# Less VectorE code in a branch that isn't taken, and another order of the first steps, in a gated cross-attention and mixture-of-experts kernel

## Chip, cores and metric

One core of a Trainium2 chip. The metric is the time of one launch in microseconds (us), the median of several runs. A core has five engines with a queue of instructions each: TensorE (PE, its weight loads PEld), VectorE (DVE), ScalarE (ACT), GpSimd (POOL) and SyncE (SP, which here only starts transfers). Waits between queues go over semaphores.

## What is computed

Eight batches of 256 rows, 512 wide. Each batch has a memory of 256 rows, of which a mask leaves some. The rows of x, normalized, attend to the memory they are left with; the result, times a gate, is added to x. Then each row goes, normalized again, to the two best of eight experts.

```
scores = einsum('bsd,bmd->bsm', layernorm(x), memory) / sqrt(D)
attn = softmax(where(mask, scores, -1e30))
x = x + tanh(g_xattn) * einsum('bsm,bmd->bsd', attn, memory)
t = layernorm(x)
probs = softmax(t @ w_router.T); top 2 of 8, weights made to sum to 1
out = sum over the two: (silu(t @ w_gate.T) * (t @ w_up.T)) @ w_down.T
x = x + tanh(g_ffn) * out
```

In these inputs a mask leaves at most 64 of a memory's 256 rows.

## The kernel before

Rows are worked in 16 tiles of 128 (NT), two to a batch; memories in four pairs of batches (NP). Matrix operands are float32.

**The start.** `m_find` numbers the unmasked rows of every memory by matmuls with a triangle of ones. For a pair p, `m_hot(p)` (VectorE, L216) makes a one-hot matrix of those numbers, `m_pick(p)` (TensorE, L224) turns it into row indices in the bank pidx, and `m_fetch(p)` (L228 on VectorE, L229 on GpSimd) adds an offset, giving gid, and gathers 2 x 64 rows of the memory into cns[p]. `m_count` finds the longest memory. Three matmuls into a bank that nobody reads (L586) keep TensorE at work.

**The branch.** All five engines load that count (L587) and branch (L589). If a memory has more than 64 rows, `long_way` handles all batches with whole memories, tile by tile and without overlap: a block of straight code on each engine. Else three loads of x are started, after ScalarE has read the gathered rows once (L594). Near the program's start, `mark_branch_hint_location` (L571) puts an instruction into the queues of TensorE and VectorE that names the branch's target in advance.

**Pairs.** `m_mean` (statistics on VectorE, L175), `m_centre` (ScalarE, L265) and `m_turn` (TensorE L272, ScalarE L273) make a pair's centred, transposed memory cT. `m_route(p)` (TensorE L279; ScalarE L281 to L283) makes the memory's router logits cw and scales cns.

**The loop over steps** (L603) is a pipeline written out by hand: each engine runs its instructions in the order in which the functions are called. In step s: `a_probs` of tile s-1 (transposed probabilities: TensorE, then ScalarE L378), `f_centre` of s-2, `a_stats` of tile s+3 (VectorE), in even steps `a_scale` (one power on GpSimd, L351), `a_scores` of tile s (TensorE L359, VectorE L363, ScalarE L366), then `a_values` of s-1 (TensorE L387, L389; VectorE L390 to L395: router logits, best two, and the sum into x). Behind follow ranking and bookkeeping of finished pairs of tiles: `f_mark`, `f_rank` (TensorE into the bank rank, VectorE, and four products ac on GpSimd, L456), `f_table` (TensorE into the bank table, L463), `f_count`, `f_weigh` (a transfer of finished rows to HBM). rank and table are started by one matmul each (L625, L626) and added to until the end of the loop. Step 0 holds extra work: the indices and gathers of pairs 1 to 3, scores of tile 1, `m_route(0)`, statistics of tiles 2 and 3, the masks `m_hide` and the constants of later steps on GpSimd.

**The banks.** Tiles of the PSUM pool share eight banks. A bank goes to a tile at its first write in the order of the program, and comes free with its last use.

**The experts.** When all rows are ranked, GpSimd gathers them by expert in lists of 128 (L677), and each list runs through its expert's matrices on TensorE (L183, L695, L710, L719); results are scattered to HBM by GpSimd (L682).

## Time and profile before

| | us |
|---|---|
| median of 3 runs | 300.76 (300.16 to 301.12) |
| the profiled execution | 298.97 |
| its span, first to last instruction | 297.2 |
| routing stage, to the first gather by expert | 92.4 |
| TensorE busy in 0 to 92.4 / 92.4 to 202 / 202 to 297.2 | 71.7 / 104.4 / 87.0 |
| VectorE busy in the same | 64.9 / 37.0 / 30.8 |
| ScalarE | 51.2 / 35.3 / 28.4 |
| GpSimd | 54.3 / 43.8 / 52.6 |

The second half of the table is from the windows of the profile. A row of the timeline below reads: start, duration, engine, line, operation, output <- inputs, shape, count, and in brackets how long the engine had been idle and who released it. Starts are counted from the first instruction. A letter q behind an engine's name (DVEq) means its queue: branches, register loads, semaphores, DMA starts.

### The profile page before, as it was taken

The page shows a single profiled execution, that of the slowest core. Times are in us where ns is not written, and L with a number is a line of the kernel's source. Part 1 is how long each engine was busy: PE and PEld are TensorE (multiplying, and loading weights), DVE is VectorE, ACT ScalarE, POOL GpSimd, SP SyncE. Part 2 cuts the span into 40 slices and gives each one's busy share as a digit, 9 for nine tenths or more (in the row PEclk, how much of TensorE's full clock was granted, in tenths as well). Part 3 has the DMA queues.
Part 4 walks back from the last instruction along what each step waited for, and adds up shares of the span by engine and source line. Part 5 has one row for each costly group of instructions (what it writes and reads, how often), then busy time and mean ns, then how long its engine had stood idle before and what let it go on. Part 6 is the DMA issues. An engine that isn't in the chain of part 4 may idle for free. (4 is left out here: it accounts for less than half of the span.)

```text
span 297.2 us, 4010 instructions
## 1 busy us (share of the span) xinstructions
PE 263.1 (89%) x1106; PEld 165.1 (56%) x1106; DVE 132.8 (45%) x450; ACT 114.8 (39%) x275; POOL 150.6 (51%) x239
## 2 busy tenths in 40 slices
PE   5587779989861999999999999999998999999990
PEld 4175568777641565555555555555554555555540
DVE  2438888887771123333333333332304334242441
ACT  2124667777770233333333333332204233333320
POOL 4528955647574403444444444443764847475252
PEclk9979999999995799999999999999999999999996
DMA  4589967999434702323323323331762655553322
GB/s 146 186 302 417 310 210 256 299 334 337 163 149 147 221 3 75 88 104 121 105 86 100 126 92 116 105 123 51 215 201 78 204 174 157 152 169 128 106 78 99
DMA packets 16078, 48.55 MB, mean 163 GB/s; under 512 B 3182, under 2 KB 3182, under 8 KB 16049
## 3 DMA queue, kind: packets, MB, share of 16 engines
q0 software_dynamic: 7984, 25.64, 27.3%
q1 hardware_dynamic: 5888, 17.85, 18.1%
q10 hardware_dynamic: 2176, 4.72, 4.1%
q8 instruction: 13, 0.21, 0.3%
q14 instruction: 17, 0.13, 0.1%
HBM read 35.08 MB, written 14.68 MB: 167 GB/s over the span
## 5 line engine op out<-in xcount | busy, mean ns | idle before, releaser
L695 PE MATMUL pgu<-wgu_sb,xT_g 128*128 x304 | 105.7, 490 | 0.9 <-ACTq L768 0.9
L695 PEld LDWEIGHTS pgu<-wgu_sb,xT_g 128*128 128x128 f32 x304 | 57.8, 192 | 49.3 <-issue 17.2
L719 PE MATMUL py<-wd_sb,hT 96*128 x152 | 71.3, 592 | 0.0
L701 DVE SCALAR_TENSOR_TENSOR th<-th,pgu 128x192 f32<-128x192 f32 x38 | 13.4, 354 | 99.1 <-ACT th L700 75.4
L682 POOL DMA_INDIRECT acc_d<-y,ids x19 | 19.3, 1016 | 59.8 <-DVE y L725 57.1
L677 POOL DMA_INDIRECT xall<-xc_d,ids x38 | 37.1, 975 | 13.1 <-issue 6.1
L700 ACT ACTIVATE th<-pgu,xall 128x192 f32<-128x192 f32 x38 | 16.0, 421 | 70.1 <-PE pgu L695 56.8
L723 ACT ACTIVATE y<-py,xall 128x512 f32<-128x512 f32 x38 | 26.1, 688 | 38.6 <-PE py L719 30.4
L719 PEld LDWEIGHTS py<-wd_sb,hT 96*128 96x128 f32 x152 | 25.9, 190 | 18.7 <-issue 18.7
L185 ACT COPY xT_g<-pt_g 128x512 f32<-128x512 f32 x38 | 22.2, 585 | 28.7 <-PE pt_g L183 16.9
L682 POOL DMA_INDIRECT out<-y,ids x19 | 19.2, 1013 | 26.5 <-DVE y L732 18.3
L456 POOL TENSOR_SCALAR ac<-cols,low,idt 128x128 f32<-128x128 f32 x30 | 25.7, 865 | 11.6 <-DVE low L446 11.6
L183 PE MATMUL pt_g<-ident,xall 128*128 128x128 f32 x152 | 23.8, 281 | 6.2 <-issue 5.6
L725 DVE SCALAR_TENSOR_TENSOR y<-xall,y 128x512 f32<-128x512 f32 x19 | 14.3, 752 | 28.8 <-ACT y L723 27.3
L677 POOL DMA_INDIRECT acc<-acc_d,ids x19 | 18.5, 975 | 8.4 <-issue 8.4
L183 PEld LDWEIGHTS pt_g<-ident,xall 128*128 128x128 f32 x152 | 18.3, 144 | 7.0 <-issue 5.9
L359 PE MATMUL psc<-cT,xT 128*128 128x137 f32 x128 | 19.0, 296 | 1.3 <-issue 0.7
L359 PEld LDWEIGHTS psc<-cT,xT 128*128 128x128 f32 x128 | 17.5, 204 | 2.0 <-issue 1.2
L710 PEld LDWEIGHTS pht<-ident,h 128*96 128x96 f32 x76 | 9.5, 126 | 14.2 <-issue 7.4
L389 PE MATMUL pav<-cn,prT 128*128 128x512 f32 x32 | 16.4, 594 | 0.0
L703 DVE SCALAR_TENSOR_TENSOR h<-th,xall,pgu 128x192 f32<-128x192 f32 x38 | 15.8, 415 | 1.4
L712 DVE COPY hT<-pht 96x256 f32<-96x256 f32 x38 | 15.8, 415 | 0.3 <-PE py L719 0.2
(156 smaller groups left out, 295.6 us busy)
## 6 DMA issues: line engine op xcount, KB each, us to landing
wgu_sb<-wgu SPq DMA_DIRECT2D x8, 768.0 KB, 9.1
xc_d<-xr ACTq DMA_DIRECT2D x8, 576.0 KB, 5.9
xT<-xT SPq DMA_DIRECT2D x8, 512.0 KB, 6.8
wd_sb<-wd SPq DMA_DIRECT2D x8, 384.0 KB, 9.4
xall<-x SPq DMA_DIRECT2D x1, 2048.0 KB
xall<-x SPq DMA_DIRECT2D x2, 512.0 KB, 3.8
xall<-x SPq DMA_DIRECT2D x1, 1024.0 KB, 8.3
xall<-xc_d,ids POOLq DMA_INDIRECT x38
```

The source lines that it names most:

```text
L183: nc.tensor.transpose(pt[:, c, :], src[:, c * P:(c + 1) * P], ident)
L185: nc.scalar.copy(dst, pt)
L359: nc.tensor.matmul(both, lhsT=xTs[b][:, c, t * P:(t + 1) * P], rhs=cTs[p % 2][:, c, :], start=(c == 0), stop=(c == HC - 1))
L389: nc.tensor.matmul(pav, lhsT=prT, rhs=cns[p], start=True, stop=True)
L456: by.tensor_scalar(at_col[:, n, :], cols, low[:, n:n + 1], idt[:, i:i + 1], ALU.is_equal, ALU.mult)
L677: nc.gpsimd.indirect_dma_start(out=g, out_offset=None, in_=src[:, :], in_offset=bass.IndirectOffsetOnAxis(ap=ids[:, q:q + 1], axis=0))
L682: free(nc.gpsimd.indirect_dma_start(out=dst, out_offset=bass.IndirectOffsetOnAxis(ap=ids[:, q:q + 1], axis=0), in_=z, in_offset=None, boun ...
L695: nc.tensor.matmul(pgu, lhsT=xgT[:, c, :], rhs=wgu_sb[:, bass.ds(v * GU + c * 2 * I, 2 * I)], start=(c == 0), stop=(c == HC - 1))
L700: nc.scalar.activation(th, pgu[:, 0:I], AF.Tanh, scale=xg[:, RS:RS + 1])
L703: nc.vector.scalar_tensor_tensor(h, th, xg[:, R2:R2 + 1], pgu[:, I:2 * I], ALU.mult, ALU.mult)
L719: nc.tensor.matmul(py, lhsT=hT[:, k, :], rhs=wd_sb[:, bass.ds(v * DN + k * D, D)], start=(k == 0), stop=(k == 1))
L723: nc.scalar.activation(y, py, AF.Copy, scale=xg[:, c:c + 1])
```

## The change

Three things.

1. In `long_way`, five instructions a tile leave VectorE. The addition of epsilon and the product of the softmax's sum with the gate go to GpSimd; the normalization, the scaling of the result and the copy of the router's part go to ScalarE. For the normalization GpSimd makes a further factor, -mean times the reciprocal deviation, in two instructions. The branch hint stays on TensorE alone.
2. In step 0, `m_route(0)` stands ahead of the pairs' indices. Only pair 1 is picked and gathered in step 0, with the statistics of tile 2 between the two. Pair 2's hot matrix stays in step 0, its pick and gather move to step 1, ahead of tile 0's values, with the hot matrix of pair 3 behind them; pair 3's pick and gather move to step 2.
3. The two matmuls that start rank and table move from step 0 to step 1, behind tile 0's values, so that their banks are given out later.

```diff
-               (("l_st", 6), ("l_mv", 2), ("l_rs", 1), ("l_vg", 1), ("l_nmx", 1), ("l_den", 1))}
-        mv, rs, vg, nmx, den = (one[k] for k in ("l_mv", "l_rs", "l_vg", "l_nmx", "l_den"))
+               (("l_st", 6), ("l_mv", 2), ("l_rs", 1), ("l_vg", 1), ("l_nmx", 1), ("l_den", 1), ("l_ng", 1))}
+        mv, rs, vg, nmx, den, ng = (one[k] for k in ("l_mv", "l_rs", "l_vg", "l_nmx", "l_den", "l_ng"))
...
-                nc.vector.tensor_scalar(mv[:, 1:2], mv[:, 1:2], EPS, None, ALU.add)
+                nc.gpsimd.tensor_scalar(mv[:, 1:2], mv[:, 1:2], EPS, None, ALU.add)
                 nc.gpsimd.tensor_tensor(rs, mv[:, 1:2], expo, ALU.pow)
+                nc.gpsimd.tensor_tensor(ng, mv[:, 0:1], rs, ALU.mult)
+                nc.gpsimd.tensor_scalar(ng, ng, -1.0, None, ALU.mult)
                 xa = row([P, D], "lx")
-                nc.vector.tensor_scalar(xa, xs[i], mv[:, 0:1], rs, ALU.subtract, ALU.mult)
+                nc.scalar.activation(xa, xs[i], AF.Identity, bias=ng, scale=rs)
...
-                nc.vector.tensor_mul(den, den, vg)
+                nc.gpsimd.tensor_tensor(den, den, vg, ALU.mult)
...
-                nc.vector.tensor_scalar(more, pav, den, None, ALU.mult)
+                nc.scalar.activation(more, pav, AF.Copy, scale=den)
...
-                nc.vector.tensor_copy(xadd[:, i, :], plg)
+                nc.scalar.copy(xadd[:, i, :], plg)
...
-        tc.mark_branch_hint_location("long", engines=[PE, DVE])
+        tc.mark_branch_hint_location("long", engines=[PE])
...
                 m_hot(1)
                 m_hot(2)
                 a_scores(1)
-                for n in range(1, 3):
-                    m_pick(n)
-                    m_fetch(n)
                 m_route(0)
-                m_hot(3)
-                m_pick(3)
-                m_fetch(3)
-                nc.tensor.matmul(rank, lhsT=ones[0:1, :], rhs=lbase, start=True, stop=True)
-                nc.tensor.matmul(table.rearrange("p k r -> p (k r)"), lhsT=ones[0:1, :], rhs=zero[:, 0:2 * P], start=True, stop=True)
+                m_pick(1)
                 a_stats(2)
+                m_fetch(1)
                 a_stats(3)
                 a_scale(1)
                 for b in range(1, B):
                     m_hide(b)
                 more_constants()
+            if 1 <= s < NP - 1:
+                m_pick(s + 1)
+                m_fetch(s + 1)
+                if s + 2 < NP:
+                    m_hot(s + 2)
             on(f_square, s - 2)
             if odd:
                 on(f_rank, (s - 3) // 2, NT // 2)
             on(a_values, s - 1)
+            if s == 1:
+                nc.tensor.matmul(rank, lhsT=ones[0:1, :], rhs=lbase, start=True, stop=True)
+                nc.tensor.matmul(table.rearrange("p k r -> p (k r)"), lhsT=ones[0:1, :], rhs=zero[:, 0:2 * P], start=True, stop=True)
```

## The prediction, made before the changed kernel was run

> **What bounds the kernel now.** First the forty slices (7.43 us each), to find stages with different limits.

> ```profile
> PE   5587779989861999999999999999998999999990
> DVE  2438888887771123333333333332304334242441
> PEclk9979999999995799999999999999999999999996
> ```

> From slice 13 on TensorE is full: the expert stage. The routing stage ahead of it (to 92.4 us, the first gather of L677) is a pipeline of TensorE, VectorE and ScalarE, and no gather can start before its last tile. Every edit lies in its first 40 us, so an edit is worth what it moves the first place where those engines meet again; all behind it shifts with it. The first three slices have idle engines. The rows of L589, the branch past the long-memory block, say why.

> ```profile
> L589 PEldq COMPARE_BRANCH  x1: 3882/3882/3882, 7.1 to 7.1; - x1
> L589 DVEq COMPARE_BRANCH  x1: 78/78/78, 10.0 to 10.0; - x1
> L589 POOLq COMPARE_BRANCH  x1: 45/45/45, 10.1 to 10.1; - x1
> ...
> L589 DVEq EVENT_SEMAPHORE  x1: 21/21/21, 12.9 to 12.9; - x1
> ```

> VectorE branches at 10.0 and issues nothing until 12.9. The profile's DMA view of 10 to 13 us holds two code packets of 8 KB (queue q14): code fetched for that jump. The timeline shows what waits.

> ```profile
> 11.15 0.19 ACT L594 COPY xall<-cn 128x1 f32<-128x1 f32 x1 [4.40 <-DMA cn<-ctxn,gid]
> ...
> 12.99 0.69 DVE L175 BATCH_NORM_STATS2 st_c<-cn 128x6 f32<-128x512 f32 x1 [3.48 <-DVEq L589]
> ...
> 16.09 3.47 PE L359 MATMUL psc<-cT,xT 128*128 128x137 f32 x16 [0.72 <-issue]
> 19.41 0.61 PE L224 MATMUL pidx<-mval,oh 128*128 128x128 f32 x4
> ...
> 36.65 1.05 PE L463 MATMUL table<-ac,ar 128*128 128x128 f32 x8
> 37.53 1.06 PE L279 MATMUL pc<-wrc,cT 128*128 128x128 f32 x8
> ```

> The gathered rows cn had landed by 11.15, when ScalarE read them; VectorE's statistics of the same rows began 1.84 later. From L175 to the scores (L359) is a bare chain: 16.09 - 12.99 = 3.10 us. The sixteen score matmuls of tiles 0 and 1 take 19.41 - 16.09 = 3.32; the eight of tile 2 take 0.95 (25.07 to 26.02 on the PE timeline). The windows give the reason:

> ```profile
> 12.06:15.47 3.41, 0.66 (x4) 0.42 (x4) 1.91 (x9) 0.78 (x2) 0.00 (x0) 1.00 0.56 170
> 15.47:18.89 3.42, 2.79 (x12) 2.83 (x13) 0.47 (x4) 0.67 (x2) 0.00 (x0) 0.50 0.95 325
> ```

> (Columns: length, busy PE, PEld, DVE, ACT, POOL, granted clock, DMA.) After a window with TensorE 0.66 us busy comes one at half clock. Last, GpSimd:

> ```profile
> 20.50 1.11 POOL L229 DMA_INDIRECT cn<-ctxn,gid  x1 [9.08 <-DVE gid L228]
> ...
> 25.25 3.96 POOL L286 TENSOR_SCALAR hide<-slot,cnt 128x64 f32<-128x64 f32 x7
> ...
> 32.67 3.42 POOL L456 TENSOR_SCALAR ac<-cols,low,idt 128x128 f32<-128x128 f32 x4
> ```

> From 20.50 to 36.09 it never rests but for 0.3 us after each gather: 15.59 us of work. Its last product, ac of pair 0, is wanted by the table matmuls at 36.65, so its slack there is half a microsecond.

> **The long-memory code.** No memory has more than 64 rows, so the block never runs here; its edits can act through the jump alone. From the code, VectorE's part is 11 instructions a tile (the reduction of L317 counts two, as L363 does in the trace) times 16, plus 3 a batch times 8: 200. Five a tile leave: 120. ScalarE goes from 80 to 128, GpSimd from 40 to 104. Waits come on top: the unchanged program as compiled has 250 VectorE instructions there, 49 of them waits; after, I estimate 150. Which length is short enough? The trace holds rows on both sides: 200 stalls 2.9 us, GpSimd's 40 doesn't (its next instructions follow at 11.4, when its running work ends). To choose: between TensorE's code packets at 109.2, 137.4, 166.7 and 196.3 us stand 254, 261 and 264 of its instructions, at 16 KB a packet, so 64 bytes each; VectorE's 8 KB packets hold 128. The jump leaves from about its 25th instruction. Before, it lands near the 276th, two packets on; after, near the 175th, in the next. I take it that the next packet is there already, and the jump costs nothing. Then L175 starts when cn lands: **-1.84 us**. The other ends: 0 if it still fetches; and with its hint gone a fetch may last as long as TensorE's hinted one, 3.88, which is 1.0 worse than 2.88.

> [...]

> The longer blocks cost nothing by their cover. ScalarE branches at 7.0 and its next work waits for cn at 11.1: a fetch like TensorE's would end at 10.9. GpSimd branches at 10.1 and next has work when gid of pair 1 is ready, 17.7 below: 7 us of cover. Without cover each would cost up to 3.9.

> **TensorE's clock.** With L175 at 11.15 the scores start at 14.25. TensorE then idles 1.4 us ahead of L272, not 3.25, and the window to 15.47 holds 0.66 + 1.22 = 1.9 us of work. The windows 42.78 to 46.19 (1.81 busy) and 83.73 to 87.15 (1.99) were followed by full clock, so I take full: 2 x 0.95 = 1.90 for 3.32, **-1.4 us**. Other end: from 15.47 at half, about 0.7 of it, and the route matmuls (L279) lose another 0.9.

> **The order in step 0.** All later steps run the same work. L279 (0.9) now stands ahead of pair 1's index matmuls, so its gid comes 0.9 later after the scores: 16.15 + 0.90 + 0.64 (19.41 to 20.05 before) = 17.7 for 20.05, and GpSimd's gather starts at 18.15. Its queue behind that keeps its sum: gathers 2 and 3 move behind the masks and constants, yet still stand before ac of pair 0. End of ac: 18.15 + 15.6 = 33.7 for 36.09. The gathers' own readers (L175 of pairs 2 and 3) come after 40 us, so they tolerate it. On VectorE the waits for the index matmuls at 21.01 and 22.35 (0.81 + 0.85) are filled by tile 2 and 3's statistics, and tile 0's logits would come some 1.4 sooner after the scores. Rows 4 to 7 of x land at 20.1 (issued 11.8, 8.3 to landing), and tile 4's statistics stand ahead of these logits in the queue: they would be reached at 18.9 and wait 1.2. That lead shrinks to about 0.4 beyond the first two terms, 3.2 + 0.4 = 3.6. Batch 2's xT lands at 29.4 and is read no sooner than 34.52 - 3.6 = 30.9: hidden. rank and table (0.85 of TensorE) go from before tile 0's transposes to behind its values: a swap at one sum. The banks: pidx lasts two steps longer, leaving five others; the bank wanted for tile 2 was read by tile 0's work long before. I cost that at 0; a wait there would be for L395, 0.7 us.

> **The sum.** At the table matmuls (36.65 before) TensorE could be 3.6 early, but the last pair needs ac at 33.7, so L279 of pair 1 follows at about 34.2 for 37.53: -3.3. I take off 0.3 for waits where two engines now arrive together: **-3.0**. The profiled execution took 298.97 us, 297.2 of it span; it would take 296.0, span 294.2. Its time is 1.8 below the median of the runs shown, 300.76, so the forecast on that scale is **297.8**. Own range 296.3 to 298.4.

> **Rivals.**
> - *The clock stays at half* (the windows' edges may fall elsewhere). Ten score matmuls fit ahead of 15.47, six follow at 0.22: the scores end at 16.9, L279 at 18.7; gid 19.3, ac 35.3, L279 of pair 1 at 35.8, so 1.7 less 0.3: 299.4. For: no window between 0.66 and 1.8 us busy is in the routing stage to compare. Chance 0.20.
> - *The jump still fetches, at today's price.* Then 1.84 and 1.4 are gone. The reordering alone frees VectorE 1.4, but GpSimd's ac ends 0.9 later, 37.0, and takes it back: 300.4 to 301.0. For: 120 lies halfway between the row that stalls and the row that doesn't. Against: the packet count. Chance 0.18.
> - *Slower: the unhinted jump.* If it fetches and lasts 3.88, L175 begins at 14.0; GpSimd's ac then ends at 36.09 + 0.9 + 1.0 = 38.0, and L279 of pair 1 follows at 38.5, 1.0 late; with the clock's window falling worse, 1.4. Time 301.8 to 302.2. It decides from the point where the jump's target isn't held. Chance 0.15.

> **How the numbers follow.** Forecast 0.47, half clock 0.20, same 0.18, slower 0.15. A change under 0.3% (0.9 us) can't be told from none here. Faster: 0.47 + 0.20 = 0.67; same 0.18; slower 0.15. The range runs from 296.2 (0.1 below the forecast's own) to 301.2 (the second rival's end): left out are the slower rival and a twentieth below.

> **What would show it.** Right: VectorE's L175 near 11.2, released by the landing of cn; TensorE's sixteen L359 matmuls in about 2 us with clock 1.00 around 15 to 19 us; GpSimd's first L456 group ending near 33.7 and TensorE waiting for it at L463; first L677 gather near 89.4. Wrong: a releaser DVEq L589 still at L175; a tile 0 whose logits wait on x for longer than 1.2 us; an idle of TensorE for a bank in steps 1 to 3; or a routing stage that ends 3 us sooner while the expert stage, whose start now falls elsewhere in the clock's windows (half clock from 90.6 to 100.8 now), gives a microsecond back or takes one.

## The result, and the profile after

The changed kernel took 300.11 us (median of 20 runs; the kernel before, run beside it, 300.79). The ratio is 0.9981, with a 95% interval of 0.9958 to 1.0005: 0.2% less, and no change isn't excluded. The forecast was 297.8 for 300.76, a ratio of 0.990. So the time lies in the forecast's range, but less than a quarter of the expected gain came. Ratios here and below leave out launches over 1.5% above the fastest of the same kernel, as three of the 20 here (303.31, 309.42 and 1540.08), though the median of 300.11 counts them. The profiled execution after took 298.80, its span 297.0 (before 298.97 and 297.2).

What the prediction asked for first was the branch past the long-memory code. In the changed file it is L591. These are its rows after: engine's queue, operation, count, three durations in ns, and when they started.

```profile
L591 PEldq COMPARE_BRANCH  x1: 3942/3942/3942, 7.0 to 7.0; - x1
L591 DVEq COMPARE_BRANCH  x1: 67/67/67, 10.0 to 10.0; - x1
...
L591 DVEq EVENT_SEMAPHORE  x1: 21/21/21, 13.1 to 13.1; - x1
```

VectorE branches at 10.0 as before and is back at 13.1, for 12.9 before: a block of 153 instructions (250 before, both counted in the compiled code) costs as much as the long one. The timeline after answers to the rows shown of before, line by line.

```profile
11.21 0.19 ACT L596 COPY xall<-cn 128x1 f32<-128x1 f32 x1 [4.36 <-DMA cn<-ctxn,gid]
...
13.22 0.69 DVE L175 BATCH_NORM_STATS2 st_c<-cn 128x6 f32<-128x512 f32 x1 [3.70 <-DVEq L591]
...
16.78 3.99 PE L361 MATMUL psc<-cT,xT 128*128 128x137 f32 x16 [0.72 <-issue]
...
22.70 1.10 POOL L229 DMA_INDIRECT cn<-ctxn,gid  x1 [11.29 <-DVE gid L228]
...
30.21 0.69 DVE L175 BATCH_NORM_STATS2 st_c<-cn 128x6 f32<-128x512 f32 x1 [0.97 <-DMA cn<-ctxn,gid]
...
34.78 3.14 POOL L458 TENSOR_SCALAR ac<-cols,low,idt 128x128 f32<-128x128 f32 x4
...
37.12 1.34 PE L465 MATMUL table<-ac,ar 128*128 128x128 f32 x8
38.30 1.06 PE L279 MATMUL pc<-wrc,cT 128*128 128x128 f32 x8
```

The rows of cn are there at 11.21, their statistics start 2.0 later, and the releaser is still VectorE's own branch. From there everything is late: the sixteen score matmuls (L361) take 3.99, pair 1's gather (L229) starts at 22.70 for 20.50, and, new, VectorE's statistics of pair 1 wait for its landing (30.21, 0.97 of waiting). GpSimd's ac of pair 0 ends at 34.78 + 3.14 = 37.92 for 36.09, and L279 of pair 1 stands at 38.30 for 37.53. The first gather by expert starts at 93.15 for 92.41.

The windows of the clock after (length; busy PE, PEld, DVE, ACT, POOL; granted clock, DMA share, GB/s):

```profile
10.63:14.04 3.41, 0.47 (x1) 0.00 (x0) 0.79 (x2) 0.19 (x1) 0.69 (x3) 1.00 0.42 144
14.04:17.45 3.41, 1.79 (x7) 1.42 (x8) 1.12 (x8) 1.31 (x2) 0.00 (x0) 0.50 1.01 339
17.45:20.87 3.42, 3.42 (x17) 3.42 (x17) 1.10 (x6) 0.44 (x2) 0.00 (x0) 0.50 0.98 323
```

TensorE is busy for 0.47 of a window, and two windows at half clock follow, where there was one before. Neither gain of the forecast's sum is there.

### The profile page after: what moved, and what is told of

Read it like the earlier page. It is cut to its first block, busy times and chain, and to the rows that moved or that the text cites. A ratio compares the mean times of both kernels' runs of the same rounds, so it can differ in the third digit from the quotient of the medians.

```text
span 297.0 us, 4010 instructions
## 1 busy us (share of the span) xinstructions
PE 265.2 (89%) x1106; PEld 167.1 (56%) x1106; DVE 133.2 (45%) x450; ACT 114.6 (39%) x275; POOL 152.8 (51%) x239
## 4 chain that ended last, share of the span: by engine, by line
PE 45%; POOL 15%; issue 15%; DMA 8%; ACT 6%; DVE 4%; ACTq 0%; POOLq 0%; another core or an unknown queue 0%
PE pgu L699 19%; PE py L723 10%; POOL out L686 5%; POOL acc L681 4%; POOL xall L681 4%; DMA xall<-xc_d,ids 4%; PE pt_g L183 3%; PE psc L361 3%; DMA cn<-ctxn,gid 3%; PE table L465 2%; PE pav L391 2%; PE pht L714 1%; PE pc L279 1%; PE ppt L389 1%; DMA acc<-acc_d,ids 1%
## 5 line engine op out<-in xcount | busy, mean ns | idle before, releaser
L699 PEld LDWEIGHTS pgu<-wgu_sb,xT_g 128*128 128x128 f32 x304 | 58.1, 192 | 49.3 <-issue 17.7
L686 POOL DMA_INDIRECT acc_d<-y,ids x19 | 19.3, 1018 | 60.4 <-DVE y L729 57.8
L681 POOL DMA_INDIRECT xall<-xc_d,ids x38 | 38.7, 1018 | 13.1 <-issue 6.2
L723 PEld LDWEIGHTS py<-wd_sb,hT 96*128 96x128 f32 x152 | 25.9, 190 | 18.7 <-issue 18.7
L686 POOL DMA_INDIRECT out<-y,ids x19 | 20.0, 1051 | 21.6 <-DVE y L736 16.1
L361 PE MATMUL psc<-cT,xT 128*128 128x137 f32 x128 | 19.6, 301 | 1.3 <-issue 0.7
L361 PEld LDWEIGHTS psc<-cT,xT 128*128 128x128 f32 x128 | 17.9, 208 | 2.0 <-issue 1.1
```

The lines of the kernel that those rows point to most:

```text
L361: nc.tensor.matmul(both, lhsT=xTs[b][:, c, t * P:(t + 1) * P], rhs=cTs[p % 2][:, c, :], start=(c == 0), stop=(c == HC - 1))
L681: nc.gpsimd.indirect_dma_start(out=g, out_offset=None, in_=src[:, :], in_offset=bass.IndirectOffsetOnAxis(ap=ids[:, q:q + 1], axis=0))
L686: free(nc.gpsimd.indirect_dma_start(out=dst, out_offset=bass.IndirectOffsetOnAxis(ap=ids[:, q:q + 1], axis=0), in_=z, in_offset=None, boun ...
L699: nc.tensor.matmul(pgu, lhsT=xgT[:, c, :], rhs=wgu_sb[:, bass.ds(v * GU + c * 2 * I, 2 * I)], start=(c == 0), stop=(c == HC - 1))
L723: nc.tensor.matmul(py, lhsT=hT[:, k, :], rhs=wd_sb[:, bass.ds(v * DN + k * D, D)], start=(k == 0), stop=(k == 1))
```

## The experiments

First theory: what counts is the length of the code that VectorE jumps over, and 153 instructions are still too many. Its rivals are named in the expectations.

**One batch and four batches of long-memory code.** The block is cut, so that memories of more than 64 rows would be handled in one or four batches only; with these inputs it isn't entered.

```diff
-        for b in range(B):
+        for b in range(1):      (in the other kernel range(4))
```

> The changed kernel with the long-memory block cut to one batch of eight (20 VectorE instructions in place of 153; the block isn't taken with these inputs). Theory 'length': VectorE's jump costs a code fetch only if its target lies beyond code that is held, so here it costs 0.3 to 0.6 us, as at L772 over 22 to 25 instructions; L175 starts when pair 0's rows land, at 11.1 to 11.4 us instead of 13.2, and the routing stage ends 2 to 3.5 us sooner: 297 to 298.5 against 300.8 before. Rival 'any jump out of the first code pays a fetch': VectorE still resumes at 12.9 to 13.1 and the time stays at 300 to 300.5.

> The changed kernel with the long-memory block cut to four batches of eight (77 VectorE instructions, not taken with these inputs). Length theory with pieces of 128 instructions of which the next is not held ahead: VectorE's jump starts near its 25th instruction and ends near its 102nd, inside the first piece if counting starts there: no stall, L175 at 11.1 to 11.4, time like the one-batch kernel. If the first piece also holds some 50 instructions of start-up code, the target is in the second piece and the stall of about 3 us remains: L175 near 13, 300 to 300.5.

With 20 instructions left, the jump takes 0.23 us (10.0 to 10.2), with 77 0.59. In both, L175 is released by the landing of cn, at 10.77 and 11.15. Times: 295.03 and 297.59 beside 300.42, ratios 0.9806 (0.9774 to 0.9838) and 0.988 (0.9841 to 0.9918). So the length of the block decides how long the jump takes, and the shorter block is worth about 1% or more; here the other engines' blocks shrank as well, which a later kernel separates. Cutting to one batch also takes TensorE's jump from 3.95 to 0.26. Its routing stage ends only 0.44 us sooner than with four batches (first gather 91.12 and 91.56), so most of the further 0.7% isn't explained by what the traces show of that stage. The profiled launch of the one-batch kernel, at 297.45, was also the slowest of its six, with the lowest granted clock (0.960; the others 0.962 to 0.977).

**Order alone, and code alone.** The kernel before with parts 2 and 3 of the change, and the kernel before with part 1.

> The kernel before with the new order of steps 0 to 2 and the later start of rank and table, and with the old long-memory code and both hints. Theory 'the order alone is the small gain': L175 at 12.9, gather of pair 1 issued about 2 us later than in the kernel before and its landing awaited by L175 of pair 1 at about 30 us; 300.0 to 300.6 against 300.8. Rival 'the order costs, the code saves': 301 to 301.8.

> The kernel before with the shorter VectorE code for long memories and no VectorE hint, in the old order. Theory 'the order alone is the small gain': VectorE still resumes at 12.9 to 13.1 and the time is that of the kernel before, 300.5 to 301.1. Rival 'the code saves': 299.8 to 300.3.

300.39 and 300.41 beside 300.42: ratios 0.9996 (0.9975 to 1.0016) and 0.9991 (0.9966 to 1.0016). Each half alone is worth nothing that can be measured; the 0.7 us between the medians after and before isn't found in either. The order alone shows its wait:

```profile
12.99 0.69 DVE L175 BATCH_NORM_STATS2 st_c<-cn 128x6 f32<-128x512 f32 x1 [3.47 <-DVEq L589]
...
23.01 1.10 POOL L229 DMA_INDIRECT cn<-ctxn,gid  x1 [11.59 <-DVE gid L228]
...
30.28 0.69 DVE L175 BATCH_NORM_STATS2 st_c<-cn 128x6 f32<-128x512 f32 x1 [0.71 <-DMA cn<-ctxn,gid]
```

**Statistics ahead of the branch.** If the jump can't be made short, can it be hidden? VectorE's statistics of pair 0 and the gates are put ahead of the load of the count, so that the jump falls while TensorE transposes; code and order of before else.

```diff
             nc.tensor.matmul(idle, lhsT=ones, rhs=busy, start=True, stop=True)
+        m_mean(0)
+        m_gates()
         v = nc.values_load(...)
...
-        m_mean(0)
         m_centre(0)
         m_turn(0)
-        m_gates()
```

> The kernel before, with old order, old long-memory code and both hints; only pair 0's statistics and the gates (VectorE) stand ahead of the branch instead of behind it. VectorE's jump still pays its fetch, now after the work that others wait for: L175 at 11.1 to 11.3 and a gap of about 3 us behind the gates, while VectorE's next work (tile 0's scores) comes near 16 to 17. Theory 'the wait for code costs only where it stands ahead of L175': the scores start 1.8 us sooner; with TensorE at half clock through them, pair 1's index comes 1 to 1.8 us sooner: 298.8 to 299.7 against 300.4. Rival 'the short jump helps in another way (less code to fetch, other engines' jumps)': no gain here, 300 to 300.8.

The ratio is 1.0064 (1.0034 to 1.0095): slower by 0.6%. Two more kernels build on it. The next has the changed kernel's order, but picks and gathers pair 1 ahead of `m_route(0)`; the third also has five idle matmuls in place of three, so that TensorE doesn't pause ahead of the scores.

```diff
                 a_scores(1)
-                m_route(0)
                 m_pick(1)
-                a_stats(2)
                 m_fetch(1)
+                m_route(0)
+                a_stats(2)
...
-        for n in range(3):      (the third kernel only)
+        for n in range(5):
```

> As the kernel with the statistics ahead, and with the new order of steps 0 to 2, but pair 1's pick and gather right behind tile 1's scores, ahead of the route matmuls. Theory 'in the new order the landing of pair 1's gather sets the routing stage, so it must start first': the gather starts 0.9 to 1.5 us sooner than with the route first, L175 of pair 1 no longer waits for it, and the time is 297 to 298.2. Rival 'GpSimd's queue up to ac of pair 0 sets it': about the same gain, as that queue starts with the gather too, but TensorE then waits at the table matmuls; the time is the same, the trace tells.

> As the gather-first kernel, with five matmuls into the unread bank instead of three (L586), so TensorE works until about 13 us. Theory of the prediction's second term: with no idle window the clock stays full through the sixteen score matmuls, which then take 1.9 to 2.2 us instead of 3.8; 1 to 1.8 us are won: 295.5 to 297. Rival 'the clock's windows fall as they do': half clock at the scores all the same, and 0 to 0.4 lost to the two extra matmuls: 297.5 to 298.5.

Ratios 1.0006 (0.9978 to 1.0034) and 1.0018 (0.9993 to 1.0043). The second kernel's timeline shows the cover that wasn't one:

```profile
11.14 0.69 DVE L175 BATCH_NORM_STATS2 st_c<-cn 128x6 f32<-128x512 f32 x1 [1.62 <-DMA cn<-ctxn,gid]
...
14.24 3.57 PE L359 MATMUL psc<-cT,xT 128*128 128x137 f32 x16 [0.72 <-issue]
...
20.50 0.28 DVE L363 CUSTOM_DVE_ANT_0 sc<-psc,hide,rs 128x64 f32<-128x64 f32 x1 [7.29 <-DVEq L591]
```

The statistics run at 11.14, but VectorE then branches at 13.69 and is back at 20.26: 6.6 us, where the jump over the same 250 instructions at 10.0 took 2.9. What differs is that x and xT are in flight then (their loads are issued from 11.4 on); that they hold up the code is likely, but no run separates it from the jump's other place in the code. The code packets on queue q14 tell a part of it. With the jump at 10.0, packets of 8 KB start at 11.04 and 11.24 in the trace before. With the jump at 13.69, only the second of them is left there (11.23), and one starts at 18.40, 1.9 before VectorE is back, as 11.04 is 1.8 before 12.9. So what grew is the time from the branch to the packet's start, from 1.0 to 4.7 us; the packets themselves take 0.3 to 0.5. In the third kernel the jump takes 5.8.

```profile
14.85 2.12 PE L359 MATMUL psc<-cT,xT 128*128 128x137 f32 x16 [0.72 <-issue]
...
19.71 0.28 DVE L363 CUSTOM_DVE_ANT_0 sc<-psc,hide,rs 128x64 f32<-128x64 f32 x1 [6.53 <-DVEq L591]
```

The idle matmuls keep the clock at 1.00, and the scores take 2.12: the forecast's second term exists. Here it is worth nothing, because VectorE, which must read the scores, is still waiting for code.

**The hint given back** to VectorE in the changed kernel (one launch).

```diff
-        tc.mark_branch_hint_location("long", engines=[PE])
+        tc.mark_branch_hint_location("long", engines=[PE, DVE])
```

> The changed kernel with VectorE's branch hint put back: 153 instructions to jump over, with a hint. Theory 'the hint starts the fetch somewhat sooner but the jump still waits for it': VectorE resumes at about 12.9 instead of 13.1. Rival 'the hint suffices for the shorter code': it resumes before 11. Second rival 'the hint does nothing': 13.1 again.

The jump goes from 10.0 to 13.1, as without it, and the launch took 298.75. The hint does nothing for the stall that can be seen.

**A block that is short and whole.** All eight batches, with VectorE left with 64 instructions. Sum and sum of squares go to ScalarE, the reciprocal, sums and products to GpSimd: 193 instructions on each (162 and 134 after the change).

```diff
-                nc.vector.bn_stats(one["l_st"], xs[i])
-                nc.vector.bn_aggr(mv, one["l_st"])
-                nc.gpsimd.tensor_scalar(mv[:, 1:2], mv[:, 1:2], EPS, None, ALU.add)
+                xa = row([P, D], "lx")
+                nc.scalar.activation(xa, xs[i], AF.Copy, scale=1.0 / D, accum_out=mv[:, 0:1])
+                nc.gpsimd.tensor_scalar(ng, mv[:, 0:1], -1.0, None, ALU.mult)
+                nc.scalar.activation(xa, xs[i], AF.Square, bias=ng, accum_out=mv[:, 1:2])
+                nc.gpsimd.tensor_scalar(mv[:, 1:2], mv[:, 1:2], 1.0 / D, EPS, ALU.mult, ALU.add)
...
-                nc.vector.reciprocal(den, den)
+                nc.gpsimd.tensor_tensor(den, den, den, ALU.mult)
+                nc.gpsimd.tensor_tensor(den, den, expo, ALU.pow)
...
-                nc.vector.tensor_add(xs[i], xs[i], more)
+                nc.gpsimd.tensor_tensor(xs[i], xs[i], more, ALU.add)
```

(The step that makes a batch's mask into an addend and one product go to GpSimd as well.) With it run the same kernel with four idle matmuls, the same with the order of before, and the changed kernel with six batches in its block, which leaves 115 instructions.

> The changed kernel with its long-memory block whole (eight batches, every step kept), but 64 instances of VectorE code in it instead of 153: sums of squares on ScalarE, reciprocal, additions and products on GpSimd (193 instructions each on ScalarE and GpSimd). Theory (only the length of VectorE's block between branch and target counts): VectorE's jump takes 0.3 to 0.7 us, statistics L175 at 11.2 released by the landing of cn, ratio to the kernel before 0.986 to 0.992, as with four batches. Rival (the gain with four batches came from the shorter blocks of the other engines, or from a shorter program): jump at 0.6 or not, the ratio stays at 0.996 or above. Second rival: ScalarE, with 193 instructions to jump over, now reads cn late (after 11.3) and takes the place of VectorE: statistics still near 11.2, but r centre later than before relative to them, ratio 0.994 to 1.0.

> The same with four idle matmuls instead of three, so that TensorE has no window with long idle time ahead of the scores. Theory (the forecast's two steps, short jump and full clock, add up): granted clock 1.00 from 11 to 20 us, the sixteen score matmuls in 2.1 us instead of 4.0, pair 1's gather at 19.0 to 19.6 instead of 21.1, ratio lower than that of the kernel with three idle matmuls by 0.004 to 0.008. Rival (what the scores gain is taken back, by GpSimd's queue of 15.6 us or by the landing of gathered rows): the clock is full and the scores take 2.1 us, but table matmuls of pair 0 end within 0.7 us of their place with three, ratio within 0.003.

> The whole short block with the order of steps of the kernel before (all of part 2 and 3 of the change undone). Theory (the new order is worth nothing in itself): ratio within 0.003 of that with the new order, 0.986 to 0.992. Rival (the new order pays once the jump is short, because it lets two chains run side by side): 0.994 to 0.998. Other rival (the new order costs, since pair 1's gather is 0.9 to 2 us later): 0.980 to 0.985, gather of pair 1 near 18.8 and its statistics without a wait for the landing.

> The changed kernel with the long-memory block cut to six batches (it isn't entered with these inputs): 115 instructions of VectorE between branch and target, where 77 took 0.59 us and 153 took 3.1. Theory (code comes in packets of 128 instructions, and the jump leaves from the 25th): the target is about the 140th, past the packet's end, so the jump takes 2.5 to 3.2 us and the ratio is 0.996 to 1.0. Rival (what counts is 128 from the branch on): 0.5 to 1.0 us, ratio 0.986 to 0.992. Third (the stall grows with the distance): 1.2 to 2.2 us.

All four ran beside the kernel before at 299.53 us.

| kernel | VectorE's instructions in the block | us | ratio (interval) |
|---|---|---|---|
| whole short block | 64 | 296.41 | 0.9895 (0.9861 to 0.9928) |
| the same, four idle matmuls | 64 | 295.12 | 0.985 (0.9814 to 0.9886) |
| whole short block, old order | 64 | 296.06 | 0.9904 (0.9871 to 0.9938) |
| six batches | 115 | 295.65 | 0.9876 (0.9837 to 0.9916) |

The branch rows of the kernel with 115 instructions:

```profile
L591 DVEq COMPARE_BRANCH  x1: 67/67/67, 10.0 to 10.0; - x1
L591 DVEq EVENT_SEMAPHORE  x1: 21/21/21, 10.6 to 10.6; - x1
```

115 instructions cost 0.6 us, as 77 and 64 do; 153 cost 3.1. The stall is a step between 115 and 153, not a slope. The theory that counted from the 25th instruction of a packet of 128 is wrong, and the count of 128 from the branch on fits VectorE, without being shown (no length between was run).

ScalarE's and GpSimd's longer blocks cost nothing that shows: in the whole short block ScalarE reads cn at 11.26. But GpSimd does stall. Its branch is at 10.1; over 134 instructions, in the changed kernel, it was back at 11.4, when its running work ended, and over 193 it is back at 13.7 (13.3 in the two kernels built on this one). Its next gather starts at 18.24 or later in all three, so that is covered. The scores' weight loads, too, now name GpSimd's branch as their releaser; but cT, the matrix that they read, is copied until 14.67, and they start at 14.74, as soon behind it as before. That 134 instructions didn't stall GpSimd also means that 128 is no count for every engine.

The timeline of the whole short block with three idle matmuls:

```profile
11.21 0.69 DVE L175 BATCH_NORM_STATS2 st_c<-cn 128x6 f32<-128x512 f32 x1 [1.69 <-DMA cn<-ctxn,gid]
...
14.77 3.99 PE L362 MATMUL psc<-cT,xT 128*128 128x137 f32 x16 [0.72 <-issue]
...
21.04 1.10 POOL L229 DMA_INDIRECT cn<-ctxn,gid  x1 [9.63 <-DVE gid L228]
...
27.52 0.69 DVE L175 BATCH_NORM_STATS2 st_c<-cn 128x6 f32<-128x512 f32 x1
...
36.66 1.06 PE L279 MATMUL pc<-wrc,cT 128*128 128x128 f32 x8
```

And with four:

```profile
11.20 0.69 DVE L175 BATCH_NORM_STATS2 st_c<-cn 128x6 f32<-128x512 f32 x1 [1.69 <-DMA cn<-ctxn,gid]
...
14.31 2.12 PE L362 MATMUL psc<-cT,xT 128*128 128x137 f32 x16 [0.72 <-issue]
...
18.24 1.10 POOL L229 DMA_INDIRECT cn<-ctxn,gid  x1 [6.83 <-DVE gid L228]
...
25.00 0.68 DVE L175 BATCH_NORM_STATS2 st_c<-cn 128x6 f32<-128x512 f32 x1
...
30.38 3.17 POOL L459 TENSOR_SCALAR ac<-cols,low,idt 128x128 f32<-128x128 f32 x4
...
33.60 0.49 PE L466 MATMUL table<-ac,ar 128*128 128x128 f32 x2 [0.31 <-POOL ac L459]
33.93 1.06 PE L279 MATMUL pc<-wrc,cT 128*128 128x128 f32 x8
```

L175 is released by the landing in both. With the fourth idle matmul the scores take 2.12, pair 1's gather starts 2.8 sooner, and L279 of pair 1 and the first gather by expert follow by as much (33.93 for 36.66; 88.76 for 91.52). So the gain isn't taken back by GpSimd's queue or by landings. The windows say what the matmul did: three idle matmuls, then four.

```profile
9.36:12.78 3.42, 1.12 (x3) 0.19 (x1) 1.62 (x8) 0.82 (x2) 1.97 (x7) 1.00 0.18 58
12.78:16.19 3.41, 2.54 (x10) 2.17 (x11) 0.45 (x3) 0.69 (x2) 0.00 (x0) 0.50 0.80 255
16.19:19.60 3.41, 3.41 (x17) 3.41 (x16) 1.84 (x9) 0.85 (x4) 0.00 (x0) 0.50 0.96 279
```

```profile
10.49:13.90 3.41, 2.06 (x8) 0.76 (x6) 1.91 (x9) 1.20 (x3) 0.83 (x3) 1.00 0.41 139
13.90:17.32 3.42, 3.01 (x26) 3.04 (x27) 1.68 (x9) 1.09 (x5) 0.00 (x0) 1.00 0.75 216
```

1.12 us busy in a window, and two at half clock follow; 2.06, and the clock stays. One profile of each would be thin evidence, as the windows' edges fell differently in these two launches (12.78 and 13.90). But the mean granted clock of all six launches with four idle matmuls is 0.972 to 0.976, of the six with three 0.961 to 0.967, and each of the former is faster than each of the latter (293.11 to 295.33 for 295.44 to 296.95).

The kernel with four idle matmuls takes 1.5% less than the kernel before; the changed kernel didn't run beside it. Its long-memory block isn't entered by these inputs, and no run here timed it.

The old order gives 0.9904 and the new 0.9895, at one short jump: the order is worth nothing there either that these intervals (0.3% each way) could show. Pair 1's gather starts at 18.90 with the old, 21.04 with the new, and GpSimd's ac of pair 0 ends at 34.53 and 36.28, but L279 of pair 1 follows at 35.97 and 36.66, and the times agree. In these two profiles the clock differs too (one window at half clock with the old order, two with the new).

## Why the prediction was wrong

**The step that failed is VectorE's jump**: "I take it that the next packet is there already, and the jump costs nothing ... -1.84 us." The block's new length (150 estimated, 153 in fact) was right; that it is short enough was not. The row was available that it costs 2.9 at 250, and another said that GpSimd's 40 (70 with its waits) don't stall; from 8 KB packets the forecast reasoned that the target's packet would be held. The runs put the step between 115 and 153 instructions. The forecast's own second rival, "The jump still fetches, at today's price" (300.4 to 301.0), is what happened: on the forecast's scale the measured ratio is 300.76 x 0.9981 = 300.2 (299.5 to 300.9). That rival's ac of pair 0 ends at 37.0; it ended at 37.92.

The evidence for it was weak in a way that could have been seen. Two 8 KB code packets at 11.04 and 11.24 were read as the fetch for that jump; in the kernel with 115 instructions such packets stand at 11.16 and 11.24, and nothing stalls there. A packet near a gap doesn't show whose it is, nor that somebody waits for it; only the kernels with the jump moved show that one of the two was VectorE's. And the trace of before held two rows that the forecast passed over: VectorE's later branches (L768) over blocks of 22 and 25 instructions, back after 0.5 us (201.6 to 202.1, 291.4 to 291.9). They show what a jump without the long stall costs, and that the only lengths known were 25 or so and 250.

**The size, where the condition holds.** With 64 to 115 instructions L175 starts at 11.1 to 11.2, as forecast, released by cn. The whole short block gives -3.1 (299.53 to 296.41) and the forecast said -3.0, but that agreement is luck: the clock's term is absent there, as the next point shows, and without it the forecast's own first rival has -1.4. With the clock's term, in the kernel with four idle matmuls, the forecast's picture is there row by row: ac of pair 0 ends at 30.38 + 3.17 = 33.55 for the 33.7 forecast, TensorE waits for it, L279 of pair 1 starts at 33.93 for 34.2, and the first gather by expert at 88.76 for 89.4. The gain is 4.4 there (299.53 to 295.12). So the path was right, and its sum too small; the last point of this section has a likely part of the reason.

**TensorE's clock** (-1.4) could not come in the changed kernel, since its cause stayed. But with the jump short it doesn't come either: the forecast's window to 15.47 would have held 1.9 us of work, while in the whole short block the window's edge fell at 12.78, 1.12 were busy ahead of it, and the scores took 3.99. That is the rival "the windows' edges may fall elsewhere", and it fell worse than that rival's one window: two. With a fourth idle matmul the term is there in full: 2.12 for 3.47 before, -1.35.

The forecast took full clock from two windows, with 1.81 and 1.99 us busy, that were followed by it. The same profile has one that speaks against so simple a test, and the forecast passed over it:

```profile
87.15:90.56 3.41, 2.24 (x12) 1.56 (x12) 1.79 (x11) 1.55 (x6) 1.71 (x3) 1.00 0.75 288
```

It holds 2.24 us of work, and half clock follows from 90.56 on. So busy time alone doesn't foretell the clock, and what does stays open.

**The order.** The forecast's figures for GpSimd hold: from pair 1's gather to the end of ac 37.92 - 22.70 = 15.2 for the 15.6 said. That this lateness is free did not: "The gathers' own readers (L175 of pairs 2 and 3) come after 40 us, so they tolerate it" left out pair 1, whose statistics wait 0.97 and 0.71 in the two kernels with the long stall and the new order. With the short jump and the new order that wait is 0.26 in the kernel with four batches, and there is none in the others. Tile 4's statistics do wait for x where the scores are early, 0.66 us at 19.70 in the kernel with four idle matmuls; the forecast had 1.2.

**The lost hint** (the slower rival, 3.88) played no part: 3.1 without and with it. The banks cost nothing that shows: no wait for one stands among the rows of steps 1 to 3.

**The profiles' own scatter.** The profiled execution of before was an early one: its first gather by expert starts at 92.41, while the four others with the long stall at 10.0 have 93.15, 93.30, 94.01 and 94.60, a mean over the five of 93.5. The five with the short jump and three idle matmuls have 90.06 to 91.56, a mean of 91.0. 2.5 us is what the jump moves on average, and one pair of profiles (92.41 and 91.52) would have shown 0.9. The profile before was lucky in its clock: one window at half clock ahead of 20 us, where each of the other four has two in a row, and a mean granted clock of 0.968, which only 3 of the 66 launches of this kernel beside the experiments reach. A forecast that starts from such a launch puts today's cost of the stall too low; that this is why the gains came out above its sum is likely, not shown.

## What to carry to other kernels

A block that never runs can still cost time through the branch past it, and on VectorE it was the number of instructions there that decided how much (3.1 us over 153, 0.59 over 115, 0.23 over 20): count them on the engine whose next work is awaited, and cut until the gap behind the branch itself falls, since a cut that ends above the step (here between 115 and 153 on VectorE) buys nothing (the code alone: 0.9991). Moving such a gap later, behind other work, can make it longer than the work that was to cover it (here 5.8 to 6.6 us at 13.7, for 2.9 at 10.0). A matmul on nothing, in TensorE's pause ahead of a chain of small matmuls, can be worth more than reordering the chain (here 1.3 us between the medians, and nothing that could be measured).
